# Softmax sums in the slot of their own logits, inverses and scaling half a slot sooner, six buffers for the recurrence's states

## The chip, the cores and the metric

The kernel runs on one core of a Trainium2 chip. The metric is device time in microseconds (us) of one execution; lower is better. The core has five engines with an instruction queue each: TensorE (PE; its weight loads appear as PEld), VectorE (DVE), ScalarE (ACT), GpSimd (POOL) and SyncE (SP), which here issues the DMAs.

## What is computed

The input x is 4 images of 128 channels and 64 x 64 pixels, fp32. Two layers follow each other.

Layer 0: a layernorm over channels, plus a 3x3 depthwise convolution with edge padding (cpe) of the same; then, in windows of 16 x 16 pixels, an attention in which each pixel looks at its 5 x 5 neighbours (zeros outside the window take part in the softmax), in 2 branches of 4 heads with 32 channels; an output projection and the residual.

```python
logits = einsum("nbhdij,nbhdkij->nbhkij", q, k_nb) * scale   # k over 25 neighbours
attn = softmax(logits, axis=3)
o = einsum("nbhkij,nbhdkij->nbhdij", attn, v_nb)
```

Layer 1, on the 4096 tokens of each image: t += cumulative linear attention of layernorm(t), with num = q . cumsum(k v), den = q . cumsum(k) + 1e-6, q and k through elu + 1; then t += recurrence, where layernorm(t) goes through a matrix and a batchnorm, and y = sigmoid(wx_t + y V^T) runs from token to token.

## The kernel before

**Tiles and stages.** The work is 16 bands (4 images x 4 rows of windows, 16 x 64 pixels each) of 4 windows, 64 "places" in all. A loop of 66 slots (lines 705 to 741) goes over the places. Slot i computes `logits(i)`: on PE a mask (L383) and 48 small matmuls (L388) into four banks, on ACT four Exp (L397) into the tiles `es0` to `es3`. Later in the slot `window_inputs` makes q, k (L343, copied from the bank on ACT at L351) and v (L356, L363, with two DMAs that lay v out anew, L365 and L366) of window i + 1.

The window before, i - 1, is finished in three pieces by the generator `weighted`: the softmax denominators as matmuls with ones (L406), their copy `den` (ACT, L409) and a DMA that packs every 32nd row into `dc` (L411); then the weighted values (48 small matmuls, L418) with the copy `o_sb` (ACT, L426); then the inverses on DVE (L429 to L433), a DMA of them to memory (`rd`, L435) and one back, spread over the partitions (`rden`, L437). Window i - 2 is scaled on POOL (`scaled`, L446: oT = o_sb * rden).

**The gaps.** Between these pieces `between(i, gap)`, gap 0 to 5, takes one step of each of two generators. `behind` is layer 1 of the band before, 24 steps (list at L618 to L643) for its two halves a and c: `output0` (output projection L471, residual L478), `measure` (L197, L199 on DVE, L201 and L202 on POOL), `norm` (L209, DVE), `turn` and `turn_last` (transposes, L218), queries, keys and values (L500 to L525, with `low` L502 on ACT, L504 and L505 on DVE), `scores` (L543, L545), `accumulate` (the running state: matmuls L560, additions L568), `attend` (L579, L581; DVE L589 to L593) and `keep` (transposes L218, copy L598, a DMA to memory L599). `product` (L608 to L610) is the matrix of the recurrence. `ahead` is `front`: the layernorm (`norm_rows`) and the convolution of later bands (`convolve`: nine `taps`, L292 on ACT and L294 on DVE, then the copy `y2w` L330 on ACT). Layer 1 of band n begins in slot 4n + 5, and its `keep` of half a falls at gap 2 of slot 4n + 8.

**What sets the order.** `in_order` (L166) ties the instructions of PE, DVE, ACT and POOL, each in the order in which the program writes them. SP is not tied. Every engine therefore waits in program order: an instruction that waits holds all that stand behind it on its engine. Slots 0 to 4 have no layer 1 to run; `ahead` alone fills their gaps. The convolution of the first band's last windows is done on PE (`multiply_first`, L312); `fourth` is the last of it, run in slot 0.

**Buffers.** Pools a1 and a2 have one and two buffers per tag; `y2`, `q`, `k`, `es`, `dc`, `o_sb` and `v_sb` come in two, `den` and `rden` in one. PE writes to 8 banks (pool ps), and a bank is free when an engine has copied what it holds.

**The end.** Slots 64 and 65 and the loop's remainder finish layer 1 of the last band. In slot 65 the pools of layer 0 are closed and `res` (all images but one, 6.3 MB) is loaded from memory for the last step. The recurrence (L826 to L860) runs 42 rounds over segments side by side, each of two halves: PE adds y V^T to a bank (L834), ACT takes the sigmoid (L847) into `ys`, from a ring of three buffers. In the 32 rounds that count POOL adds the residual to 24 of 32 columns and DVE to 8 (L854), and a DMA writes them out (L860). Checks of the recurrence's warm-up follow (L865 to L893).

```python
            sums = weighted(windows[i - 1]) if 1 <= i <= len(places) else iter(())
            for gap in (1, 2):
                next(sums, None)
                between(i, gap)
            run(sums)
```

Of the kernel before, what the change touches and what calls it, by code (L numbers as in the profile page):

```python
# [17 lines left out]
P = 128  # L18
# [28 lines left out]
def conv_attn_hybrid(ctx: ExitStack, tc: tile.TileContext, ins: dict, out: bass.AP):  # L47
# [276 lines left out]
    def convolve(n, half):  # L324

        y = ypads[n] if half == 0 else ypads.pop(n)
        y2 = a2.tile([P, WS, 2 * WS], F32, tag="y2", name="y2")
        yield from taps(y2, y, half * 2 * WS, 2 * WS, 1 + half)
        y2w = a2.tile([P, 2, WT], F32, tag="y2w", name="y2w")
        nc.scalar.copy(  # L330
            y2w.rearrange("p n (r c) -> p n r c", c=WS),
            y2.rearrange("p r (n c) -> p n r c", c=WS),
        )
        y2s[n, half] = y2w

    def window_inputs(w, n, wj):
# [3 lines left out]
        for name, wT in (("q", wqT), ("k", wkT)):  # L340
            pps = bank()
            for br in range(BR):
                nc.tensor.matmul(  # L343
                    pps[:, br * WT : (br + 1) * WT],
                    wT[:, br * P : (br + 1) * P],
                    y2,
                    start=True,
                    stop=True,
                )
            w[name] = a2.tile([P, BR * WT], F32, tag=name, name=name)  # L350
            nc.scalar.copy(w[name], pps)  # L351
            yield
# [46 lines left out]

    def weighted(w):  # L400


        ops, dps = bank(), bank()
        for h in range(HEADS):
# [4 lines left out]
        nc.scalar.copy(den, dps)  # L409
        dc = a2.tile([P, 16], F32, tag="dc", name="dc")  # L410
        nc.sync.dma_start(dc, den[::HD, :])  # L411
        yield
        for br, n in pieces:
            cols, _ = spans(br, n)
            for h in range(HEADS):
# [8 lines left out]
                )  # L424
        o_sb = a2.tile([P, BR * WT], F32, tag="o_sb", name="o_sb")
        nc.scalar.copy(o_sb, ops)  # L426
        yield

        nc.vector.tensor_tensor(dc, dc, pad_c, ALU.add)  # L429
        rc = a2.tile([P, 16], F32, tag="rc", name="rc")  # L430
        nc.vector.reciprocal(rc, dc)
        nc.vector.tensor_tensor(dmax, dmax, dc, ALU.max)
        nc.vector.tensor_tensor(dmin, dmin, dc, ALU.min)  # L433
        rd = dram4.tile([HEADS, BR * WT], F32, tag="rd", name="rd")
        nc.sync.dma_start(rd.rearrange("h (a e) -> (h a) e", e=16), rc)  # L435
        rden = a1.tile([P, BR * WT], F32, tag="rden", name="rden")
        nc.sync.dma_start(rden, rd.unsqueeze(1).to_broadcast([HEADS, HD, BR * WT]))  # L437
        w["o"], w["rden"] = o_sb, rden
        yield

# [111 lines left out]
    def accumulate(h):  # L552

        h.states = [states.get(h.b)]
        for e in range(2):
            dps = bank()
            ds = [dps[:, i * (P + 1) : (i + 1) * (P + 1)] for i in range(2)]
            for i, d in enumerate(ds):
# [4 lines left out]
            for d in ds:  # L563
# [5 lines left out]
                h.states.append(new)  # L569
        states[h.b] = h.states.pop()  # L570

# [133 lines left out]
    for i in range(len(places) + 2):  # L705
        if i < len(places):
            n, wj = places[i]
            if i and wj == 0 and n + 1 < len(bands) and bands[n + 1][1] < NB - 1:
                load_head(n + 2)
            logits(windows[i])  # L710
        if 2 <= i:
            m, wjm = places[i - 2]
            if wjm == NB - 1:
                run(behind)
                behind = layer1(m, halves.pop(m - 1, (None, None)))
        between(i, 0)
        if 2 <= i:
            scaled(m, wjm, windows.pop(i - 2))
        if i == len(places) + 1:
            layer0.close()  # L720
            early = fast.enter_context(tc.tile_pool(name="early", bufs=1))
            res = early.tile([P, B - 1, NH, SEG, HSEGS], F32, name="res")
            for b in range(B - 1):
                nc.sync.dma_start(res[:, b].rearrange("p n s k -> p n (s k)"), resd[b])
        if i < len(places) and wj == 1 and n + 2 < len(bands):
            load(n + 2)
        sums = weighted(windows[i - 1]) if 1 <= i <= len(places) else iter(())
        for gap in (1, 2):
            next(sums, None)
            between(i, gap)  # L730
        run(sums)
        if i == 0:
            run(fourth)
        inputs = iter(())
        if i + 1 < len(places):
            windows[i + 1] = {}
            inputs = window_inputs(windows[i + 1], *places[i + 1])
        for gap in (3, 4, 5):
            next(inputs, None)
            between(i, gap)  # L740
        run(inputs)
    run(behind)
    run(layer1_end(*halves.pop(len(bands) - 1)))
# [68 lines left out]

    last = ring.tile([P, COLS], F32, tag="ys", name="ys")
    for c0, c1 in halves:
# [11 lines left out]
    for r, (s, counts) in enumerate(rounds):  # L826
        seed(r // 2 + ZBUFS - 1, r % 2)

        moved, were_moved = rounds[r] == (SEG - 1, False), rounds[r] == (0, True)
        ys = None if moved else ring.tile([P, COLS], F32, tag="ys", name="ys")  # L830
        for g, (c0, c1) in enumerate(halves):
# [729 lines left out]
```

## Time and profile before

| what | value |
|---|---|
| median of 6 runs | 928.7 us (926.81 to 931.01) |
| the profiled execution | 925.04 us |
| its span, first to last instruction | 923.3 us |
| mean granted PE clock | 0.982 |
| PE, DVE, ACT, POOL busy | 95%, 79%, 58%, 28% of the span |
| first mask matmuls of slots 0 to 4 (L383) | 23.43, 32.71, 39.01, 45.38, 52.15 us |
| logits of slot 5 (L388) | 64.48 us |
| distance of bands (first L471 of a band: 226.14, 276.58, 326.45, 377.25) | some 50.3 us |
| last sums (L406) | 805.86 us |
| first output projection of the last band (L471) | 820.64 us |
| first and last addition of the recurrence on POOL (L854) | 875.00 and 912.7 us |

In the rows that follow, L12 is line 12 of the kernel before. A row has a start in us, a length in us, the engine, the line, the operation, output <- inputs, and how many instructions it gathers; in brackets stands how long the engine had been idle and what ended it. A PE that is "busy" may still run at half clock; the granted clock is a column of its own.

### The profile page before, as it was taken

To read this page: it belongs to the slowest core of one execution; us is meant where nothing else is said; L and a number is where in the kernel's file an instruction comes from. 1 tells how busy PE (TensorE), PEld (TensorE's weight loads), DVE (VectorE), ACT (ScalarE), POOL (GpSimd) and SP (SyncE) were. 2 spreads that over 40 slices of the span, in tenths; PEclk is the share of its full clock that TensorE was granted. 3 is DMA by queue.
4 is the path that set the end of the run, shared out by engine and by line. 5 is a ranking of instruction groups with operands and counts; after the bars stand their busy time and mean duration, and the time that the engine had idled before them with its cause. 6 is when DMAs were issued, how large, how long until landed. Compare 5 with 4: busy or idle time off the path is not lost.

```text
span 923.3 us, 26463 instructions
## 1 busy us (share of the span) xinstructions
PE 872.8 (95%) x10507; PEld 652.0 (71%) x10508; DVE 732.6 (79%) x2408; ACT 539.6 (58%) x1010; POOL 259.7 (28%) x358
## 2 busy tenths in 40 slices
PE   4978999999999999999999999999999999977894
PEld 3756777877777877777787777777777778656452
DVE  6465979888897978798888879787979887577684
ACT  3755566565756565665656575656666565623463
POOL 2122230413232232314132323223231412131195
PEclk9988999999999999999999999999999999999798
DMA  4111121121212111212112121212121111153154
GB/s 122 34 43 56 49 72 37 54 57 58 60 63 57 52 55 49 74 38 72 46 50 61 60 60 49 64 50 67 49 72 38 55 38 49 40 204 154 75 218 150
DMA packets 53189, 63.46 MB, mean 69 GB/s; under 512 B 22976, under 2 KB 33856, under 8 KB 52416
## 3 DMA queue, kind: packets, MB, share of 16 engines
q1 hardware_dynamic: 51616, 61.10, 21.0%
q8 instruction: 85, 1.39, 0.6%
q10 hardware_dynamic: 1440, 0.57, 0.3%
q14 instruction: 48, 0.39, 0.1%
HBM read 35.44 MB, written 17.30 MB: 57 GB/s over the span
## 4 chain that ended last, share of the span: by engine, by line
PE 57%; DVE 28%; ACT 5%; POOL 4%; issue 4%; DMA 2%; ACTq 0%; POOLq 0%; DVEq 0%; SPq 0%
DVE y L294 10%; PE bank L343 8%; PE bank L471 6%; PE bank L388 6%; PE bank L218 6%; PE bank L500 4%; PE bank L406 4%; PE bank L356 4%; PE bank L418 3%; PE bank L608 3%; DVE st L197 2%; PE z L834 2%; DVE f L505 2%; PE bank L579 2%; DVE state L568 2%
## 5 line engine op out<-in xcount | busy, mean ns | idle before, releaser
L294 DVE SCALAR_TENSOR_TENSOR y<-ypad,cpe_w,y 128x512 f32<-128x512 f32 x240 | 192.3, 801 | 15.0 <-ACT y L292 11.5
L397 ACT ACTIVATE es<-bank 128x512 f32<-128x512 f32 x256 | 132.2, 603 | 77.1 <-PE bank L388 77.1
L446 POOL TENSOR_TENSOR oT<-o_sb,rden 128x512 f32<-128x512 f32 x64 | 83.1, 1298 | 244.1 <-DMA rden<-rd 191.2
L201 POOL TENSOR_SCALAR rs<-mv 128x4 f32<-128x4 f32 (+2 forms) x100 | 25.0, 250 | 364.7 <-DVE mv L199 161.2
L209 DVE TENSOR_SCALAR xn<-x,mv,rs 128x128 f32<-128x128 f32 x256 | 90.0, 412 | 26.5 <-POOL rs L202 26.5
L202 POOL TENSOR_TENSOR rs<-rs,mhalf 128x4 f32<-128x4 f32 (+2 forms) x100 | 106.3, 1063 | 8.3
L388 PEld LDWEIGHTS bank<-q,k 32*128 32x128 f32 x3072 | 97.7, 189 | 7.6 <-ACT k L351 6.4
L388 PE MATMUL bank<-q,k 32*128 32x96 f32 (+1 forms) x3072 | 96.3, 270 | 1.1 <-ACT k L351 1.1
L418 PEld LDWEIGHTS bank<-es,v_sb 128*32 128x32 f32 x3072 | 56.6, 110 | 30.2 <-issue 17.1
L471 PE MATMUL bank<-woT,oT 128*128 128x128 f32 x512 | 65.6, 282 | 5.4 <-POOL oT L446 5.4
L500 PE MATMUL bank<-xl,awT 128*128 128x512 f32 x128 | 70.0, 630 | 0.0
L418 PE MATMUL bank<-es,v_sb 128*32 128x96 f32 (+1 forms) x3072 | 69.9, 239 | 0.0
L406 PE MATMUL bank<-es,ones 128*32 128x512 f32 x512 | 69.1, 612 | 0.0
L471 PEld LDWEIGHTS bank<-woT,oT 128*128 128x128 f32 x512 | 62.3, 196 | 9.5 <-POOL oT L446 7.1
L363 ACT COPY v_sb<-bank 128x512 f32<-128x512 f32 x64 | 37.5, 586 | 53.5 <-PE bank L356 46.8
L343 PE MATMUL bank<-y2w,wqT 128*128 128x256 f32 x256 | 66.4, 382 | 1.1 <-DVE y2w L294 1.1
L343 PE MATMUL bank<-y2w,wkT 128*128 128x256 f32 x256 | 65.8, 380 | 0.0
L356 PE MATMUL bank<-wvT,y2w 128*128 128x256 f32 x256 | 65.8, 380 | 0.0
L351 ACT COPY q<-bank 128x512 f32<-128x512 f32 x64 | 37.6, 588 | 41.0 <-PE bank L343 39.0
L351 ACT COPY k<-bank 128x512 f32<-128x512 f32 x64 | 37.4, 584 | 36.8 <-PE bank L343 36.7
L197 DVE BATCH_NORM_STATS2 st<-x 128x6 f32<-128x128 f32 x256 | 55.5, 280 | 1.1
L343 PEld LDWEIGHTS bank<-y2w,wqT 128*128 128x128 f32 x256 | 45.8, 194 | 12.8 <-issue 7.2
(118 smaller groups left out, 1714.0 us busy)
## 6 DMA issues: line engine op xcount, KB each, us to landing
rden<-rd SPq DMA_DIRECT2D x64, 256.0 KB
v_sb<-v_sb SPq DMA_DIRECT2D x128, 64.0 KB
resd<-rs_o SPq DMA_DIRECT2D x32, 256.0 KB
out<-ot SPq DMA_DIRECT2D x32, 256.0 KB
xin<-in_xt SPq DMA_DIRECT2D x15, 512.0 KB
res<-resd SPq DMA_DIRECT2D x3, 2048.0 KB
late<-resd SPq DMA_DIRECT2D x2, 1024.0 KB
dc<-den SPq DMA_DIRECT2D x64, 8.0 KB
```

Source lines behind the costliest of these rows:

```text
L202: nc.gpsimd.tensor_tensor(rs[:, :n], rs[:, :n], mhalf[:, :n], ALU.pow)
L209: nc.vector.tensor_scalar(xn[:, j, :], piece, mv[:, j, 0:1], rs[:, j : j + 1], ALU.subtract, ALU.mult)
L294: nc.vector.scalar_tensor_tensor(y2, src, cpe_w[:, tap : tap + 1], y2, ALU.mult, ALU.add)
L343: nc.tensor.matmul(pps[:, br * WT : (br + 1) * WT], wT[:, br * P : (br + 1) * P], y2, start=True, stop=True,)
L356: nc.tensor.matmul(vps[:, e * 256 : (e + 1) * 256], y2[:, e * P : (e + 1) * P], wvT, start=True, stop=True,)
L388: nc.tensor.matmul(sps[h][:, cols], w["k"][rows, k0 : k0 + P], w["q"][rows, cols], start=False, stop=(br, n) == pieces[-1],)
L397: nc.scalar.activation(es, sps[h], AF.Exp, scale=scale)
L406: nc.tensor.matmul(dps[rows], ones[:, :HD], w["es", h], start=True, stop=True)
L418: nc.tensor.matmul(ops[rows, cols], w["v"][:, n, c0 : c0 + HD], w["es", h][:, cols], start=(br, n) == pieces[0], stop=(br, n) == pieces[-1],)
L446: nc.gpsimd.tensor_tensor(oTs[n][:, :, :, wj * WS : (wj + 1) * WS], w["o"].rearrange("p (a r c) -> p a r c", a=BR, c=WS), w["rden"].rearra ...
L471: nc.tensor.matmul(yps[:, j * P : (j + 1) * P], oT[:, br, t], woT[:, br, :], start=br == 0, stop=br == BR - 1,)
L500: nc.tensor.matmul(zps, awT[:, m * P : (m + 1) * P], h.xl, start=True, stop=True)
```

## The change

`weighted` is cut into three functions. `sums(i)` (denominators, den, dc's DMA) is now called in slot i itself, between gap 2 and the inputs of the next window. `weighted(i - 1)` keeps the weighted values and o_sb and stands between gap 1 and gap 2. `inverses(i)` (DVE, and the two DMAs of rd and rden) stands in slot i behind v of the next window, ahead of gap 5. `scaled(i - 1)` stands in slot i behind gap 4, where `scaled(i - 2)` stood behind gap 0. The pools of layer 0 are so closed, and res loaded, in slot 64 rather than 65. The load of a later band's x keeps its place behind gap 0.

Besides: `y2`, `q` and `k` have one buffer instead of two; `accumulate` leaves out the last of the four state updates in the last half of each image, where nothing reads the state; `ys` has six buffers.

```diff
--- before.py
+++ after.py
@@ -324,7 +324,7 @@
     def convolve(n, half):
 
         y = ypads[n] if half == 0 else ypads.pop(n)
-        y2 = a2.tile([P, WS, 2 * WS], F32, tag="y2", name="y2")
+        y2 = a1.tile([P, WS, 2 * WS], F32, tag="y2", name="y2")
         yield from taps(y2, y, half * 2 * WS, 2 * WS, 1 + half)
         y2w = a2.tile([P, 2, WT], F32, tag="y2w", name="y2w")
         nc.scalar.copy(
@@ -347,7 +347,7 @@
                     start=True,
                     stop=True,
                 )
-            w[name] = a2.tile([P, BR * WT], F32, tag=name, name=name)
+            w[name] = a1.tile([P, BR * WT], F32, tag=name, name=name)
             nc.scalar.copy(w[name], pps)
             yield
         vps = bank()
@@ -397,19 +397,35 @@
             nc.scalar.activation(es, sps[h], AF.Exp, scale=scale)
             w["es", h] = es
 
-    def weighted(w):
-
-
-        ops, dps = bank(), bank()
+    def sums(w):
+
+        dps = bank()
         for h in range(HEADS):
             rows = slice(h * HD, (h + 1) * HD)
             nc.tensor.matmul(dps[rows], ones[:, :HD], w["es", h], start=True, stop=True)
 
         den = a1.tile([P, BR * WT], F32, tag="den", name="den")
         nc.scalar.copy(den, dps)
-        dc = a2.tile([P, 16], F32, tag="dc", name="dc")
-        nc.sync.dma_start(dc, den[::HD, :])
-        yield
+        w["dc"] = a2.tile([P, 16], F32, tag="dc", name="dc")
+        nc.sync.dma_start(w["dc"], den[::HD, :])
+
+    def inverses(w):
+
+        dc = w["dc"]
+
+        nc.vector.tensor_tensor(dc, dc, pad_c, ALU.add)
+        rc = a2.tile([P, 16], F32, tag="rc", name="rc")
+        nc.vector.reciprocal(rc, dc)
+        nc.vector.tensor_tensor(dmax, dmax, dc, ALU.max)
+        nc.vector.tensor_tensor(dmin, dmin, dc, ALU.min)
+        rd = dram4.tile([HEADS, BR * WT], F32, tag="rd", name="rd")
+        nc.sync.dma_start(rd.rearrange("h (a e) -> (h a) e", e=16), rc)
+        w["rden"] = a1.tile([P, BR * WT], F32, tag="rden", name="rden")
+        nc.sync.dma_start(w["rden"], rd.unsqueeze(1).to_broadcast([HEADS, HD, BR * WT]))
+
+    def weighted(w):
+
+        ops = bank()
         for br, n in pieces:
             cols, _ = spans(br, n)
             for h in range(HEADS):
@@ -422,21 +438,8 @@
                     start=(br, n) == pieces[0],
                     stop=(br, n) == pieces[-1],
                 )
-        o_sb = a2.tile([P, BR * WT], F32, tag="o_sb", name="o_sb")
-        nc.scalar.copy(o_sb, ops)
-        yield
-
-        nc.vector.tensor_tensor(dc, dc, pad_c, ALU.add)
-        rc = a2.tile([P, 16], F32, tag="rc", name="rc")
-        nc.vector.reciprocal(rc, dc)
-        nc.vector.tensor_tensor(dmax, dmax, dc, ALU.max)
-        nc.vector.tensor_tensor(dmin, dmin, dc, ALU.min)
-        rd = dram4.tile([HEADS, BR * WT], F32, tag="rd", name="rd")
-        nc.sync.dma_start(rd.rearrange("h (a e) -> (h a) e", e=16), rc)
-        rden = a1.tile([P, BR * WT], F32, tag="rden", name="rden")
-        nc.sync.dma_start(rden, rd.unsqueeze(1).to_broadcast([HEADS, HD, BR * WT]))
-        w["o"], w["rden"] = o_sb, rden
-        yield
+        w["o"] = a2.tile([P, BR * WT], F32, tag="o_sb", name="o_sb")
+        nc.scalar.copy(w["o"], ops)
 
     oTs = {}
 
@@ -552,9 +555,10 @@
     def accumulate(h):
 
         h.states = [states.get(h.b)]
+        count = 4 - (h.hb == NH - 1)
         for e in range(2):
             dps = bank()
-            ds = [dps[:, i * (P + 1) : (i + 1) * (P + 1)] for i in range(2)]
+            ds = [dps[:, i * (P + 1) : (i + 1) * (P + 1)] for i in range(min(2, count - 2 * e))]
             for i, d in enumerate(ds):
                 j = 2 * e + i
                 nc.tensor.matmul(
@@ -567,7 +571,7 @@
                 else:
                     nc.vector.tensor_tensor(new, h.states[-1], d, ALU.add)
                 h.states.append(new)
-        states[h.b] = h.states.pop()
+        states[h.b] = h.states[-1]
 
     def attend(h, e):
 
@@ -703,7 +707,8 @@
             next(ahead, None)
 
     for i in range(len(places) + 2):
-        if i < len(places):
+        inside, after = i < len(places), 1 <= i <= len(places)
+        if inside:
             n, wj = places[i]
             if i and wj == 0 and n + 1 < len(bands) and bands[n + 1][1] < NB - 1:
                 load_head(n + 2)
@@ -714,31 +719,36 @@
                 run(behind)
                 behind = layer1(m, halves.pop(m - 1, (None, None)))
         between(i, 0)
-        if 2 <= i:
-            scaled(m, wjm, windows.pop(i - 2))
-        if i == len(places) + 1:
-            layer0.close()
-            early = fast.enter_context(tc.tile_pool(name="early", bufs=1))
-            res = early.tile([P, B - 1, NH, SEG, HSEGS], F32, name="res")
-            for b in range(B - 1):
-                nc.sync.dma_start(res[:, b].rearrange("p n s k -> p n (s k)"), resd[b])
-        if i < len(places) and wj == 1 and n + 2 < len(bands):
+        if inside and wj == 1 and n + 2 < len(bands):
             load(n + 2)
-        sums = weighted(windows[i - 1]) if 1 <= i <= len(places) else iter(())
-        for gap in (1, 2):
-            next(sums, None)
-            between(i, gap)
-        run(sums)
+        between(i, 1)
+        if after:
+            weighted(windows[i - 1])
+        between(i, 2)
+        if inside:
+            sums(windows[i])
         if i == 0:
             run(fourth)
         inputs = iter(())
         if i + 1 < len(places):
             windows[i + 1] = {}
             inputs = window_inputs(windows[i + 1], *places[i + 1])
-        for gap in (3, 4, 5):
-            next(inputs, None)
-            between(i, gap)
+        next(inputs, None)
+        between(i, 3)
+        next(inputs, None)
+        between(i, 4)
+        if after:
+            scaled(*places[i - 1], windows.pop(i - 1))
+        if i == len(places):
+            layer0.close()
+            early = fast.enter_context(tc.tile_pool(name="early", bufs=1))
+            res = early.tile([P, B - 1, NH, SEG, HSEGS], F32, name="res")
+            for b in range(B - 1):
+                nc.sync.dma_start(res[:, b].rearrange("p n s k -> p n (s k)"), resd[b])
         run(inputs)
+        if inside:
+            inverses(windows[i])
+        between(i, 5)
     run(behind)
     run(layer1_end(*halves.pop(len(bands) - 1)))
     in_order(first)
@@ -810,7 +820,7 @@
     nc.gpsimd.memset(warm[:, :, 0:1], 0.0)
     halves = [(0, GC), (GC, COLS)]
 
-    last = ring.tile([P, COLS], F32, tag="ys", name="ys")
+    last = ring.tile([P, COLS], F32, tag="ys", name="ys", bufs=6)
     for c0, c1 in halves:
         nc.scalar.activation(
             last[:, c0:c1].rearrange("p (m k) -> p m k", k=HSEGS),
@@ -827,7 +837,7 @@
         seed(r // 2 + ZBUFS - 1, r % 2)
 
         moved, were_moved = rounds[r] == (SEG - 1, False), rounds[r] == (0, True)
-        ys = None if moved else ring.tile([P, COLS], F32, tag="ys", name="ys")
+        ys = None if moved else ring.tile([P, COLS], F32, tag="ys", name="ys", bufs=6)
         for g, (c0, c1) in enumerate(halves):
             b = slice(c0 // SEGS, c1 // SEGS)
             z = seeds[r // 2, g][:, r % 2, :]
```

## The prediction

> **What bounds the kernel now.** I read the busy shares first, then TensorE (PE) by windows of time, then the rows in which PE waited, then the queue of VectorE (DVE) and GpSimd (POOL) round the two long waits, and the chain of waits for the end.
>
> ```profile
> PE 872.8 (95%) x10507; PEld 652.0 (71%) x10508; DVE 732.6 (79%) x2408; ACT 539.6 (58%) x1010; POOL 259.7 (28%) x358
> ```
>
> The windows, each with its length, then busy time (and count) of PE, weight loads, DVE, ScalarE (ACT) and POOL, the granted PE clock, DMA share and GB/s:
>
> ```profile
> 40.00:65.00 25.00, 19.82 (x348) 14.30 (x348) 15.97 (x42) 15.52 (x30) 4.50 (x5) 0.93 0.18 51
> 65.00:100.00 35.00, 32.66 (x419) 24.03 (x412) 21.22 (x64) 19.50 (x36) 8.23 (x12) 0.86 0.17 53
> ...
> 300.00:400.00 100.00, 99.21 (x1286) 76.05 (x1285) 84.86 (x288) 61.71 (x113) 28.44 (x41) 1.00 0.19 55
> ...
> 600.00:700.00 100.00, 99.94 (x1287) 76.09 (x1286) 85.14 (x287) 62.21 (x114) 27.55 (x38) 1.00 0.19 56
> ...
> 800.00:840.00 40.00, 33.09 (x304) 25.01 (x301) 30.34 (x106) 12.71 (x22) 8.58 (x11) 1.00 0.47 186
> ```
>
> Between 100 and 800 us PE is the bound: the seven windows leave 3.5 us idle. There a change pays only if it removes matmuls, and costs as soon as it makes PE wait. Room lies at both ends. PE's rows at its longest waits (start, length, line; in brackets the idle time and its releaser):
>
> ```profile
> 63.02 0.58 PE L383 MATMUL bank<-mask_q,mask_k 32*128 32x512 bf16 x1 [4.12 <-ACT den L409]
> 64.48 2.89 PE L388 MATMUL bank<-q,k 32*128 32x96 f32 x48 [0.88 <-ACT k L351]
> ...
> 74.83 3.63 PE L471 MATMUL bank<-woT,oT 128*128 128x128 f32 x16 [2.34 <-POOL oT L446]
> ```
>
> ```profile
> 820.64 2.05 PE L471 MATMUL bank<-woT,oT 128*128 128x128 f32 x16 [2.47 <-POOL oT L446]
> ```
>
> POOL's rows before the last of them:
>
> ```profile
> 818.35 1.01 POOL L202 TENSOR_TENSOR rs<-rs,mhalf 128x4 f32<-128x4 f32 x1
> 819.33 1.26 POOL L446 TENSOR_TENSOR oT<-o_sb,rden 128x512 f32<-128x512 f32 x1
> ```
>
> The scaling of window 63 sits behind a layernorm's power (L202) in POOL's order, although its inverses were issued long before.
>
> **The change, part by part** (against the profiled execution, 925.04 us; span 923.3 us. The median of the six runs, 928.7, is 3.7 above it, and I add that at the end.)
>
> *Start-up, slots 0 to 5.* Here nothing of layer 1 fills PE. Removed: the 4.12 us are not a wait for the sums as such. ACT runs its list in order; y2w (L330) stands in front of den, o_sb and the q, k, v copies, and waits 5.87 us for the convolution taps on DVE (L294), which end at 61.83. A bank for the mask matmul comes free only when den is copied. After, the same copies still stand behind y2w. Moreover DVE reaches the taps later: the inverses of the slot's own window stand in DVE's order before the last gap's taps, and wait for a dc that was issued only behind the previous window's rden on SP. In the rows before, dc lands 1.9 us after issue when alone (62.99 to 64.86) and about 4 us after it when behind an rden (43.37 to 47.18); DVE's three waits for it before 62 us are 0.83, 2.41 and 3.14. I get taps that end at 64.0 to 64.3, 2.3 later. Added: PE's sums now need the slot's own Exp. Four Exp take 2.06 us from 0.1 us behind the logits. In slot 0 only 18 convolution matmuls (25.06 to 29.14) could cover them, and these stand behind the sums, so PE waits about 1.65; in slots 1 to 4 the 1.07 us of weighted matmuls and little else lie between, which leaves about 0.6 in each: 4 us together, most of which shortens the wait for the taps that follows. Gained: oT of window 3 is no longer late, so the 2.34 us go, and with them part of the slow clock. From 63.02 to 78.25 PE took 15.2 us, of which 3.2 idle in the two waits at 64.48 and 74.83 and 6.9 the work of those blocks at full-speed durations (L388 1.48 for 2.89, L406 1.06 for 1.94, L471 2.05 for 3.63): 5.1 us are the clock. If logits of slot 5 start at about 67 (64.48 + 2.3) with PE warm, PE reaches the place of 78.25 at 76.6; with another cold stretch at 78.1, or, if dc lands still later, at 81. I take **0** (bounds -3 and +3): a later start traded for a warm clock and a wait removed.
>
> The granted clock in 2 us rows was 0.50 from 62 to 70 after the wait of 4.12, 0.50 at 76 to 78 after the one of 2.34, and 1.00 right through the one of 2.47 at 818 to 820.6. The Trainium skill ("TensorE: Matmul & The Clock Gate", section "What's actually happening") says that the clock halves after an idle window of some 3.4 us and that the window runs free. By that rule waits split into pieces of 0.6 would never cool PE, and the start-up term here would be -1.6 rather than 0; the row with 0.50 after only 2.34 speaks against counting on it.
>
> *The middle, slots 6 to 63.* Removed: the last of four state updates in the last half of each batch (4 times): two passes of 0.13 us each on PE, 4 x 2 x 0.13 = 1.06 us, of which one lies in the tail: **-0.8**. Its DVE additions (0.29 each) lie beside PE. Three waits of 0.21 for oT (175.87, 377.25, 578.43): **-0.6**. Moved: the sums (8 passes, 1.06 us) go from behind gap 0 to behind gap 2 of the slot. They are covered by everything between, because Exp ends 2.1 us after the logits and gaps 0, 1 and weighted hold over 3 us of PE. But in the fourth slot of a band gap 2 is where `keep` of half a turns x; PE meets it 1.06 us earlier, and its wait for x from DVE, already there, grows:
>
> ```profile
> 363.98 0.58 PE L218 MATMUL bank<-ident,x 128*128 128x128 f32 x2 [0.35 <-DVE x L593]
> ```
>
> DVE is unbroken from 350.82 to 376, so x comes sooner only by what its start gains: `low` at 350.82 waited 1.80 for ACT, where den's copy (0.6) stood directly ahead. It gains about 0.5, so PE loses 1.06 - 0.5 = 0.55 a band. Against that, the inverses (366.79 to 367.24, 0.45 us on DVE) no longer stand ahead of xn (L209), for which the transposes at 368.98 took 1.01 rather than 0.60: -0.45 a band. Over 14 bands 14 x 0.1 = **+1.4**. SP: rden's issues go behind v_sb's, so v, read a whole slot later, lands sooner; the scaling that reads rden has half a slot from there. y2, q and k with one buffer each: their readers (y2w's copy, the logits) stand before the next writer in every order, so 0; if not, one ACT copy of 0.59 per slot would show. Middle: 0.0 (bounds -3 and +4; for +10 see the rivals).
>
> *The tail, from the last logits on.* PE loses sums(63) from 805.86 (0.99 to the next start) and DVE the inverses at 810.77 (1.49 to the next start, slow because POOL's L446 of 810.65 runs beside it). State L568, behind those inverses, held PE 0.48 at 812.60 and xn 0.90 at 813.99. So x of half c, ended at 816.93, ends 2 us sooner; oT(63) is scaled a slot sooner and its place on POOL is free, so output0 follows the product instead of waiting 2.47. What is late next is DVE: statistics, rs (1.3), xn (1.11 alone, not the 2.04 it took beside the scaling), statistics L610 (0.69), then x15 at 819.1 to 819.5 instead of 822.73: **-3.3** (bounds -1.5 and -4.5; the loads of res, 6.3 MB, start a slot sooner, and in SP's order stand before the stores of the last rows, which are not due before 841.98). The fourth skipped update: **-0.3**. The rest up to the recurrence is one chain, which moves as a whole.
>
> *The recurrence.* Rounds start 1.17 us apart until ACT's wait for the ring begins, then 1.22. In front of these sigmoids stands an event wait:
>
> ```profile
> L847 ACTq EVENT_SEMAPHORE  x29: 642/788/790, 876.9 to 911.0; - x29
> ```
>
> With six buffers its readers are older, but the instruction still names POOL and PE, so one such wait stays. The least gain is three rounds that begin without it, 3 x 0.05 = 0.15, the most 29 x 0.045 = 1.3. POOL's addition (1.10 a round) fits below 1.17 too. **-0.4**, nearer the lower end, because ACT at 877.58 started before DVE's addition of 877.31 had ended, so the readers were not what held it.
>
> Sum: 0 + 0.0 - 3.3 - 0.3 - 0.4 = -4.0: 925.04 becomes 921.0, and the median 928.7 - 4.0 = **924.7 us**.
>
> **Rivals.** *A, the start-up gains too.* PE stays warm, both long waits go, slot 5 is reached as early as 61: -3 there, -1.3 in the recurrence, -4.5 at the tail: 917 to 921 in runs. For it: 7.3 us of idle and 5.1 of slow clock lie there. Against: the taps, which set the 4.12, do not move earlier.
>
> *B, no change that can be measured.* The measurement tells some 0.3% (2.8 us) from nothing. The later taps cost 2 to 3 us in full while the tail gives 3: 926 to 930, at 928. For it: DVE's waits for dc are in the rows of before already; the changed order adds one queue ahead of dc.
>
> *C, slower: `keep` meets DVE.* If `low` does not move by 0.5 (ACT's Exp hold it instead) and POOL's scaling, now in gap 4 or 5, slows DVE's inverses as it did at 810.77 (1.18 for 0.14), every band costs the full 1.06 on PE: 14 x 1.06 = +14.8, less 0.45 x 14 = 6.3 and less 0.8 + 0.6 + 4.0 in the rest: about +3; with the collision of 1.04 in one window of each band +14 x 0.5 more: **932 to 939**, at 935. It decides as soon as the wait at `keep` exceeds 0.9 us a band. Against: DVE has 14 to 15 us of slack in each 100.
>
> *D, six buffers do not do what they say*: the round stays at 1.22. That costs the forecast 0.4 and no more; it is within its range.
>
> **How the numbers follow.** Forecast 0.42 (922 to 927), A 0.18, B 0.20, C 0.20. Limits are 925.9 and 931.5. Faster: 0.75 of the forecast and all of A: 0.50. Same: the rest of the forecast and 0.9 of B: 0.28. Slower: C and the rest: 0.22. The range leaves out the lower tenth (half of A) and the upper (half of C): 918 to 934.
>
> **What would show it.** Right: PE's wait at `keep` of half a is 0.7 to 1.1 a band, and the transposes of `turn_last` take 0.6; no PE wait for oT is left; in the first 62 us PE waits for ACT's es in front of the sums, 1.6 once and about 0.6 in four slots; the taps before slot 5 end at 64; the first output0 of the last band starts at 816 to 817. Wrong: band starts more than 0.3 us further apart than 50.3 (rival C), a wait on PE for es or dc after slot 6, or rounds at 1.17 throughout (recurrence -1.3).

## The result: 934.0 us, slower where a small gain was forecast

The changed kernel's median is 934.02 us over 18 runs (930.08 to 938.39); the kernel before, run beside it, has 928.57 us over 39 (925.61 to 931.73). The ratio is 1.0058, 95% interval 1.0045 to 1.007: about 5.4 us lost, where 4.0 were to be won. Two more measurements gave 1.005 (1.003 to 1.0069) and 1.0088 (1.0058 to 1.0117). The profiled execution took 939.66 us, with a span of 937.6.

The windows of the changed kernel's trace (length; busy time and count of PE, weight loads, DVE, ACT, POOL; granted PE clock; DMA share; GB/s), to set beside those of before:

```profile
40.00:65.00 25.00, 25.00 (x392) 16.23 (x380) 14.21 (x23) 17.87 (x34) 3.58 (x3) 1.00 0.17 45
65.00:100.00 35.00, 30.38 (x371) 22.61 (x371) 24.67 (x82) 18.73 (x34) 10.51 (x15) 0.95 0.18 53
...
300.00:400.00 100.00, 97.21 (x1254) 74.62 (x1256) 82.13 (x279) 59.34 (x110) 28.02 (x41) 0.98 0.18 54
...
600.00:700.00 100.00, 98.78 (x1279) 75.09 (x1271) 83.86 (x283) 62.04 (x114) 26.46 (x38) 1.00 0.19 56
...
800.00:840.00 40.00, 37.58 (x453) 28.91 (x451) 26.38 (x100) 17.90 (x32) 9.62 (x13) 1.00 0.26 92
```

PE is no longer full in the middle: from 100 to 800 us it is busy 685.8 us instead of 696.6. The new idle time is nearly all in one place. PE's rows there in two bands of the changed kernel:

```profile
270.03 0.59 PE L218 MATMUL bank<-ident,x 128*128 128x128 f32 x2 [1.35 <-DVE x L597]
...
680.12 0.59 PE L218 MATMUL bank<-ident,x 128*128 128x128 f32 x2 [0.45 <-DVE x L597]
```

This is `keep` of half a, at gap 2 of a band's fourth overlapped slot: PE wants to turn x, which DVE has not finished. It waited 0.2 to 0.44 us there before. In the changed kernel the waits of 0.2 us and more sum to 14.0 us over the bands, against 2.4 before.

Stage by stage I use four marks: slot 0's first mask matmul, the first output projection of band 1, of band 14 and of band 15. "Before's order" are the kernel before and three kernels below that keep its order of the sums; "changed" are three profiles of the changed kernel.

| stage | before's order (4 profiles) | changed (3 profiles) | difference of means |
|---|---|---|---|
| slot 0 to band 1 | 101.6 to 104.0 | 102.8, 102.9, 103.1 | +0.2 |
| band 1 to band 14 | 649.9 to 653.1 | 666.7, 664.4, 664.6 | +13.7 |
| band 14 to band 15 | 42.1 to 43.2 | 39.3, 39.3, 39.3 | -3.5 |
| band 15 to the end of the span | 102.7 to 106.4 | 103.6, 103.4, 103.7 | -0.3 |

The stages sum to some 10 us, the timed runs to 5.4 to 8 or so. The three profiled executions of the changed kernel (939.66, 937.87, 937.93 us) lie 3 to 6 us above their timed medians, those of before's order between 3.5 below and 3 above. Why is open; the stages show where time goes, the ratios how much.

### The profile page after: what moved, and what is told of

Its sections match the earlier page's. It is cut to its first block, busy times and chain, and to the rows that moved or that the text cites. A ratio compares the mean times of both kernels' runs of the same rounds, so it can differ in the third digit from the quotient of the medians.

```text
span 937.6 us, 26498 instructions
## 1 busy us (share of the span) xinstructions
PE 882.0 (94%) x10499; PEld 655.1 (70%) x10500; DVE 733.2 (78%) x2404; ACT 539.2 (58%) x1010; POOL 254.8 (27%) x358
## 4 chain that ended last, share of the span: by engine, by line
PE 77%; DVE 16%; issue 2%; ACT 2%; DMA 1%; POOL 1%; ACTq 0%; DVEq 0%; POOLq 0%
PE bank L343 12%; PE bank L405 8%; PE bank L218 7%; PE bank L388 7%; PE bank L503 6%; PE bank L474 6%; DVE y L294 6%; PE bank L434 6%; PE bank L356 5%; PE z L844 4%; PE bank L612 3%; PE bank L520 3%; PE bank L546 2%; PE bank L383 2%; DVE x L597 2%
## 5 line engine op out<-in xcount | busy, mean ns | idle before, releaser
L294 DVE SCALAR_TENSOR_TENSOR y<-ypad,cpe_w,y 128x512 f32<-128x512 f32 x240 | 197.9, 825 | 12.0 <-ACT y L292 9.0
L209 DVE TENSOR_SCALAR xn<-x,mv,rs 128x128 f32<-128x128 f32 x256 | 82.0, 382 | 32.0 <-POOL rs L202 31.9
L202 POOL TENSOR_TENSOR rs<-rs,mhalf 128x4 f32<-128x4 f32 (+2 forms) x100 | 98.9, 989 | 8.3
L405 PE MATMUL bank<-es,ones 128*32 128x512 f32 x512 | 76.3, 617 | 0.7 <-ACT es L397 0.7
L343 PE MATMUL bank<-y2w,wqT 128*128 128x256 f32 x256 | 74.7, 415 | 1.0 <-DVE y2w L294 1.0
L503 PE MATMUL bank<-xl,awT 128*128 128x512 f32 x128 | 67.6, 612 | 0.0
L474 PE MATMUL bank<-woT,oT 128*128 128x128 f32 x512 | 64.7, 280 | 0.0
L474 PEld LDWEIGHTS bank<-woT,oT 128*128 128x128 f32 x512 | 61.8, 194 | 3.6 <-issue 0.8
L408 ACT COPY den<-bank 128x512 f32<-128x512 f32 x64 | 37.9, 592 | 40.3 <-PE bank L405 39.3
```

The lines of the kernel that those rows point to most:

```text
L202: nc.gpsimd.tensor_tensor(rs[:, :n], rs[:, :n], mhalf[:, :n], ALU.pow)
L209: nc.vector.tensor_scalar(xn[:, j, :], piece, mv[:, j, 0:1], rs[:, j : j + 1], ALU.subtract, ALU.mult)
L294: nc.vector.scalar_tensor_tensor(y2, src, cpe_w[:, tap : tap + 1], y2, ALU.mult, ALU.add)
L343: nc.tensor.matmul(pps[:, br * WT : (br + 1) * WT], wT[:, br * P : (br + 1) * P], y2, start=True, stop=True,)
L405: nc.tensor.matmul(dps[rows], ones[:, :HD], w["es", h], start=True, stop=True)
L474: nc.tensor.matmul(yps[:, j * P : (j + 1) * P], oT[:, br, t], woT[:, br, :], start=br == 0, stop=br == BR - 1,)
```

## The experiments

**The changed kernel twice more**, for further profiles (no edit).

> The changed kernel once more, for a second profile. Theory K (PE meets keep of half a 1.06 us earlier in each band and waits for x from DVE): ratio to before 1.004 to 1.008, PE's wait at keep summed over the bands 8 to 14 us, and a wait over 1.2 us followed now and then by a stretch at half clock, which would explain why the profiled run (939.66) lies 5.6 above the median. Theory S (the loss is in the start-up, slots 0 to 5): the wait at keep differs from run to run and does not carry the difference; the start-up is 5 us or more later than before.

> The changed kernel a third time, for its profile: PE's wait at keep summed over the bands 8 to 16 us, from 0.3 to 1.4 in a band; the bands with 1.2 us or more are those in which POOL's scaling starts inside a pair of taps of that slot (2.4 us for the pair instead of 1.53). Rival: the sum is under 6 us where the execution takes 934 or less.

Medians 934.66 and 935.03 us. The waits at `keep` of 0.2 us and more sum to 15.3 and 14.3 us (the first profile, 14.0): 1.0 to 1.1 in a band. The rival of few waits is out. The start-up theory is out by the table. What sets the wait's size is seen in DVE's rows ahead of `keep`. First the band with the long wait, then one with the short, both from the changed kernel:

```profile
256.56 0.43 DVE L507 TENSOR_SCALAR low<-low 128x512 f32<-128x512 f32 x1 [0.67 <-ACT low L505]
...
257.69 1.53 DVE L294 SCALAR_TENSOR_TENSOR y<-ypad,cpe_w,y 128x512 f32<-128x512 f32 x2
259.69 0.69 DVE L528 TENSOR_TENSOR v<-bank,abv 128x512 f32<-128x512 f32 x1 [0.47 <-PE bank L520]
260.30 2.45 DVE L294 SCALAR_TENSOR_TENSOR y<-ypad,cpe_w,y 128x512 f32<-128x512 f32 x2
```

```profile
667.75 0.43 DVE L507 TENSOR_SCALAR low<-low 128x512 f32<-128x512 f32 x1 [0.67 <-ACT low L505]
...
670.70 0.69 DVE L528 TENSOR_TENSOR v<-bank,abv 128x512 f32<-128x512 f32 x1 [0.30 <-PE bank L520]
671.31 1.53 DVE L294 SCALAR_TENSOR_TENSOR y<-ypad,cpe_w,y 128x512 f32<-128x512 f32 x2
```

Two things differ: the wait of `v` for PE (0.47 and 0.30), and a pair of taps that takes 2.45 us instead of 1.53. The slow pair lies beside POOL's scaling, which starts when rden lands (260.94 to 262.20 here; in the second band at 672.82, behind the taps). In the first and third profiles of the changed kernel all 15 waits of 1.0 us or more go with a pair of 2.08 to 2.63 us, and the shorter ones with pairs of 1.53 to 2.07; in the second one wait of 1.18 goes with 2.04. This tells the long waits from the short ones, not the changed kernel from the kernel before: there the pair beside POOL took 2.2 to 2.6 us in each of the eight bands whose wait shows. Only the last band waits 0.31 with 2.42: no statistics of a later band stand between the two additions of x there.

The expectation also linked long waits to half clock. Only some show it. The changed kernel's windows after the wait of 1.36 us that ended at 321.61:

```profile
320.00:322.00 2.00, 0.64 (x4) 0.33 (x3) 1.93 (x14) 0.09 (x1) 0.91 (x2) 1.00 0.24 85
322.00:324.00 2.00, 2.00 (x10) 0.36 (x11) 2.00 (x13) 0.62 (x2) 1.25 (x3) 0.59 0.30 114
324.00:326.00 2.00, 2.00 (x7) 1.64 (x8) 0.25 (x4) 0.58 (x2) 1.82 (x4) 0.55 0.22 75
```

The granted clock falls to about half for some 3.4 us and the band takes 52.67 us; after the wait of 1.35 at 270.03 it stayed at 1.00. Of 20 waits of 1.3 us or more in the three profiles, three had such a stretch behind them (two, none and one), so it is a small part of the loss.

**Sums ahead of gap 2**, so that PE does them before it comes to `keep`, as it did before:

```diff
         if after:
             weighted(windows[i - 1])
-        between(i, 2)
         if inside:
             sums(windows[i])
+        between(i, 2)
```

> The changed kernel with sums(i) ahead of gap 2 instead of behind it, so that PE again does the sums before it turns x for keep. Theory K: PE's wait at keep of half a falls back to 0.2 to 0.5 us a band (from 1.0 on average), 0.7 to 1.0 x 14 = 10 to 14 us less than the changed kernel in the profile, 918 to 925 us, faster than before. Theory S: no change against the changed kernel, 931 to 935.

918.03 us, ratio 0.986 (0.9832 to 0.9887). One pair of lines turns +0.6% into -1.4%: 16 us. The waits at `keep` fall to 6.3 us in all, as theory K said, yet they are not what was won, since 6.7 us of new waits for xn stand at `turn_last`. Between the marks of band 1 and band 14 PE is idle for 11.5 us, against 12.9 to 14.6 in the three profiles of the changed kernel, and busy for 636.3 us, against 649.8 to 653.3. So the time came where K put it for another reason: in the profile PE's matmuls took some 13 us less. That is the theory W of a later run: sums now stand directly behind the weighted matmuls, both with 32-column weights. PE's rows in this kernel:

```profile
229.09 1.09 PE L434 MATMUL bank<-es,v_sb 128*32 128x96 f32 x48
230.00 1.04 PE L405 MATMUL bank<-es,ones 128*32 128x512 f32 x8
230.97 2.05 PE L474 MATMUL bank<-woT,oT 128*128 128x128 f32 x16
232.86 1.03 PE L343 MATMUL bank<-y2w,wqT 128*128 128x256 f32 x4
```

and the same stretch of the changed kernel:

```profile
230.39 1.09 PE L434 MATMUL bank<-es,v_sb 128*32 128x96 f32 x48
231.41 2.05 PE L474 MATMUL bank<-woT,oT 128*128 128x128 f32 x16
233.39 1.06 PE L405 MATMUL bank<-es,ones 128*32 128x512 f32 x8
234.39 1.13 PE L343 MATMUL bank<-y2w,wqT 128*128 128x256 f32 x4
```

From start to start, q's matmuls take 0.86 us behind other 128-column work and 0.96 behind the sums (234.39 to the next row at 235.35): 0.1 us for the passage out of small weights (a passage is a change between groups with 32-column or 32-row weights and groups with 128x128 ones). L474 stands behind small weights in both kernels, and in the changed kernel ahead of them too: 1.98 instead of 1.89, so 0.09 for the passage into them. With those of the logits a band has 16 passages here and 24 in the kernel before and the changed one. Over the 13 bands between the marks that is 104 fewer, some 10 of the 13 us.

**`keep` one step later**, with the sums where the change has them:

```diff
-            (scores, c), (keep, a), None,
-            (accumulate, c), (norm, a), None,
+            (scores, c), None,
+            (accumulate, c), (norm, a), (keep, a), None,
```

> The changed kernel with keep of half a one step of layer 1 later (with accumulate c and norm a, gap 3 instead of gap 2); the sums stay behind gap 2 and so come before keep. Theory K: the wait at keep is gone (below 0.2 a band) with the sums where the change put them, 10 to 14 us less in the profile, 918 to 925. A rival K2 (not keep's place but the sums' own wait or switch on PE costs the time): the time stays within 2 us of the changed kernel's, 932 to 936.

928.68 us, ratio 0.9994 (0.9973 to 1.0015). No wait at `keep` is left, and about 6 us are regained, not 10 to 14. K2 is out, and K holds with a smaller size: `turn_last` waits for xn instead, up to 0.89 us in a band (all waits shown sum to 6.3), since DVE is not done sooner. The middle takes 657.4 us, half way between 665 and 652; PE is idle for 6.6 us of it and busy for 650.8.

**The pair behind gap 2, with `keep` late**: `keep_late` with weighted moved from ahead of gap 2 to directly ahead of the sums.

```diff
         between(i, 1)
+        between(i, 2)
         if after:
             weighted(windows[i - 1])
-        between(i, 2)
         if inside:
             sums(windows[i])
```

> The changed kernel with keep of half a one step later (as in keep_late) and weighted(i - 1) moved behind gap 2, directly ahead of sums(i), so that the two groups of 32-column matmuls are one group in each slot. Theory K alone (the wait at keep is the whole loss of the middle): the same as keep_late, 927 to 930. Theory K + W (each passage between 32-column and 128-column weights costs PE about 0.1 us; two fewer in a slot, 8 fewer in a band): 1.0 to 1.4 us a band less than keep_late without PE's waits, 14 x 1.0 to 1.4 = 14 to 20 less if no new wait appears, 910 to 918.

920.49 us, ratio 0.9913 (0.9887 to 0.9939): 8 us better than `keep_late`, less than the 14 to 20. K alone is out. In the middle PE is busy for 639.2 us instead of 650.8: 11.6 us for 104 passages, or 0.11 for one, as the rows above have it. Its idle time grows from 6.6 to 13.7 us, most of it for xn, so some 60% of what the passages save is given back to DVE. W holds, at some 0.1 us a passage; why PE takes that time, no run shows.

**Sums behind q and gap 3.** PE reaches `keep` as early as in the changed kernel, but L520, for which DVE's `v` waits, comes sooner (5.97 us behind its slot's masks instead of 7.16).

```diff
         between(i, 2)
-        if inside:
-            sums(windows[i])
...
         next(inputs, None)
         between(i, 3)
+        if inside:
+            sums(windows[i])
```

> The changed kernel with sums(i) one step later still, behind q and gap 3 of the slot (and in slot 0 behind fourth). PE turns x for keep at the same place as in the changed kernel, ahead of the sums, but reaches the values of half c (L520), for which DVE's v has to wait 0.3 to 0.7 us a band in the changed kernel and not at all before, 1.06 us sooner. Theory V (low's 0.5 us on DVE were gained as predicted and then lost again in this wait): v's wait for L520 goes, x comes 0.5 us sooner and PE's wait at keep falls to 0.4 to 0.9 a band; with the first slots' sums behind q (3 us) some 5 to 9 us less than the changed kernel, 925 to 929. Rival: x does not move, since the taps beside POOL's scaling set it; the wait at keep stays at 1.0 on average, 931 to 935.

924.86 us, ratio 0.998 (0.9963 to 0.9997); the changed kernel, measured beside it, had 1.0088. The wait lists (total, times, longest) have the wait of `v`, first the changed kernel's, then this one's:

```profile
DVE v L528 <- PE bank L520: 11.3, 16, 1.8
```

```profile
DVE v L528 <- PE bank L520: 2.3, 2, 1.7
```

In the middle, waits at `keep` fall from 14.3 to 7.1 us with the slow taps still there (2.1 to 2.6 us in all ten bands shown). So theory V holds: the wait of `v` for PE, not POOL's collision alone, keeps x late. No run takes the collision away, so what it adds to the other half is not shown. The first slots changed too (sums behind q), but the first stage takes 102.4 us, hardly less; the middle takes 653.1.

**Ahead's steps at odd gaps**, in the changed kernel:

```diff
-        if i < len(places) and (i == 0 or i % NB or gap in (0, 2, 4)):
+        if i < len(places) and (i == 0 or i % NB or gap in (1, 3, 5)):
```

> The changed kernel, sums where it has them, with the steps of ahead in the first slot of a band taken at gaps 1, 3 and 5 instead of 0, 2 and 4. The statistics of a later band's x (L197 and L199, 1.2 us on DVE) then stand behind the second addition of attend a instead of ahead of it. Theory K (what PE waits for at keep is DVE's queue): the wait at keep falls by 1.0 to 1.2 us a band to at most 0.3, 12 to 14 us less in the middle, 920 to 925. Rival: DVE is late at the next place by as much (turn_last's xn behind the same statistics), so the wait only moves there and the time stays within 3 us of 934.

934.79 us, ratio 1.0047 (1.0031 to 1.0063): as the rival said. The wait at `keep` falls as K said, to 0.3, and a new one stands 10 us later. PE's rows:

```profile
267.00 0.59 PE L218 MATMUL bank<-ident,x 128*128 128x128 f32 x2 [0.31 <-DVE x L597]
...
276.94 1.00 PE L218 MATMUL bank<-ident,xf 128*128 128x128 f32 x4 [0.45 <-DVE xf L209]
```

The waits shown in the middle sum to 10.0 us instead of 14: 4.8 for xf, 1.8 for x, and 3.3 that the profile puts down to ACT's Exp. The time is the changed kernel's. A piece of DVE's queue moved only moved the wait.

**The first slots' sums later**, on top of sums ahead of gap 2, and the same with ahead's steps at odd gaps (`best_odd`, which adds the edit just shown):

```diff
-        between(i, 2)
-        if inside:
+        if inside and 5 <= i:
             sums(windows[i])
+        between(i, 2)
         if i == 0:
             run(fourth)
+            sums(windows[i])
...
         next(inputs, None)
+        if 1 <= i < 5:
+            sums(windows[i])
         between(i, 3)
```

> sums_before_gap2 with the sums of slot 0 behind the last convolution matmuls (fourth) and those of slots 1 to 4 behind q of the next window, so that PE has work while ACT takes Exp. Theory X (PE's waits for es in the first five slots, seen as sums of 2.3 to 2.5 us instead of 1.06, some 7.8 us together, set when slot 5 begins): logits of slot 5 start 3 us or more sooner, 914 to 916. Theory T (the convolution taps on DVE set it, through y2w on ACT): PE waits longer ahead of slot 5's masks instead and slot 5's logits move by less than 2 us, 916.5 to 919.

> start_later with the same move of ahead's steps. Theory K: the wait of 0.5 to 1.0 at keep goes, 0.4 to 0.6 a band, 5 to 9 us less than start_later, 907 to 911. Rival (the wait moves to turn_last's xn, which already waits 0.35 to 0.7 a band): within 2 us of start_later, 914 to 918.

915.82 us, ratio 0.9871 (0.9835 to 0.9908), and 914.84 us, ratio 0.9828 (0.98 to 0.9857). Against sums ahead of gap 2 (0.986) `start_later` is not distinct. Its logits of slot 5 start 42.0 us after slot 0's masks instead of 45.2, while PE waits 2.66 instead of 0.36 at the masks of slot 5: X and T both see part of what happens. `best_odd` is where its rival put it. These are the fastest kernels of the study, 1.3 to 1.7% below the kernel before.

**Parts alone, on the kernel before.** Six buffers:

```diff
-    last = ring.tile([P, COLS], F32, tag="ys", name="ys")
+    last = ring.tile([P, COLS], F32, tag="ys", name="ys", bufs=6)
...
-        ys = None if moved else ring.tile([P, COLS], F32, tag="ys", name="ys")
+        ys = None if moved else ring.tile([P, COLS], F32, tag="ys", name="ys", bufs=6)
```

> The kernel before with six buffers for ys and nothing else. My prediction's step: 0.15 to 1.3 us less, rounds still with an event wait ahead of most sigmoids. Rival: nothing (rounds at 1.22 after the warm-up, as before), or all of it (rounds of 1.17 throughout, 1.3 us less). All three lie within 0.2%: the time alone will not tell, the spacing of the sigmoids will.

928.03 us, ratio 0.9982 (0.9967 to 0.9997). The interval just excludes no gain, yet the trace shows no place for 1.6 us: rounds start 1.17 us apart until the ring wait begins, then 1.23 to 1.24, where the three-buffer ring had 1.22 to 1.23. The row of the sigmoids' event wait, of this kernel:

```profile
L847 ACTq EVENT_SEMAPHORE  x26: 17/17/17, 887.1 to 918.2; - x26
```

The wait is met at once (17 ns), yet each round is 0.06 longer from its first use on. That points to the further wait itself as the price, not to a reader that is late; no run takes the wait away. Three fewer such rounds save 0.15, and 26 that are 0.01 longer cost 0.3.

The skipped update:

```diff
+        count = 4 - (h.hb == NH - 1)
...
-            ds = [dps[:, i * (P + 1) : (i + 1) * (P + 1)] for i in range(2)]
+            ds = [dps[:, i * (P + 1) : (i + 1) * (P + 1)] for i in range(min(2, count - 2 * e))]
...
-        states[h.b] = h.states.pop()
+        states[h.b] = h.states[-1]
```

> The kernel before with the fourth state update left out in the last half of each image, nothing else. My prediction's step: PE 8 passes of 0.13 us fewer, 1.1 us less in all (ratio 0.9988). Rival: nothing, since DVE or the tail's chain hides it (ratio 1.000). They lie 0.12% apart, so the time may not decide; the bands that hold an image's last half should be 0.27 us shorter than the others by their output projections.

926.64 us, ratio 0.9989 (0.9968 to 1.0011). The middle value is the one forecast, but the interval holds the rival too; the time did not decide. The bands with a last half (from bands 3, 7 and 11 to the next) took 49.8 us on average, and 50.4 in the kernel before; that leans to the step, but bands scatter by as much.

The scaling sooner:

```diff
         between(i, 0)
-        if 2 <= i:
-            scaled(m, wjm, windows.pop(i - 2))
...
-        for gap in (3, 4, 5):
+        for gap in (3, 4):
             next(inputs, None)
             between(i, gap)
+        next(inputs, None)
+        if 1 <= i <= len(places):
+            scaled(*places[i - 1], windows.pop(i - 1))
...
+        between(i, 5)
         run(inputs)
```

> The kernel before with the scaling alone moved: scaled(i - 1) behind gap 4 and v of slot i instead of scaled(i - 2) behind gap 0 of the next, and res loaded one slot sooner; sums, inverses and all else as before. My prediction's step on the tail: most of the 3.3 us come from oT(63) being ready, so the first output projection of the last band starts 1.5 to 3 us sooner, and the three 0.2 us waits for oT go: 925.5 to 928. Rival: rden lands after the scaling's new place and holds POOL, and with it the layernorms' rs behind it: the middle gets longer, 929 to 934.

928.09 us, ratio 0.9997 (0.9975 to 1.0018). The tail still waits, as PE's row shows:

```profile
822.51 3.39 PE L471 MATMUL bank<-woT,oT 128*128 128x128 f32 x16 [2.02 <-POOL oT L446]
```

The stage is 42.1 us, 1.1 less than the kernel before's 43.2, not 39.3. The tail's gain in the changed kernel is therefore not the scaling's place alone. The skipped update alone has 42.7 there; for the rest the sums and inverses out of slot 64 are what is left, and no run moves them by themselves. POOL was not held by it in the middle (650.9 us).

## Why the prediction was wrong, point by point

**The step that failed: the middle, forecast 0.0, and in it the +1.4 of 14 bands x (1.06 - 0.5 - 0.45).** The middle measured +13.7 us in the profiles. The place was named, PE at `keep` of half a, and the sign given for it even came true: the wait is 1.0 to 1.1 a band, within 0.7 to 1.1. So did the sign of rival C, since bands start 51.1 to 51.3 us apart on average. In the timed runs, which lost 5.4 us in all, the middle must be smaller: an estimate is 5.4 + 3.6 for the tail, some 9 us. What went wrong is the price. The row of before that the forecast started from, 0.35, was one of the longer ones (2.4 us in 14 bands is 0.17 a band), so the wait grew by 0.83 to 0.92 a band and not by 0.55, and the 0.45 that was to pay for it did not come.

The first half of the working held. In the band read here (masks of the slot ahead of `keep` at 244.91 us before, at 251.44 after) PE came to `keep` 16.84 us behind these masks instead of 18.03: the sums' 1.0 from start to start, and two passages. `low` on DVE started 0.48 us sooner (5.60 us behind its slot's masks before, 5.12 after) where 0.5 were forecast. The failure is in "x comes sooner only by what its start gains. It gains about 0.5". Between `low` and x stands `v`, which reads PE's L520, and L520 sits 7.15 us behind its slot's masks in both kernels. DVE, 0.48 sooner, waited there 0.47. DVE's rows of before, to set beside the first ones of the changed kernel above:

```profile
251.64 2.42 DVE L294 SCALAR_TENSOR_TENSOR y<-ypad,cpe_w,y 128x512 f32<-128x512 f32 x2
...
254.46 0.68 DVE L525 TENSOR_TENSOR v<-bank,abv 128x512 f32<-128x512 f32 x1
...
263.11 0.61 DVE L593 SCALAR_TENSOR_TENSOR x<-bank,rd,x 128x128 f32<-128x128 f32 x2
```

I had taken DVE to be unbroken because its rows of before showed no wait; they showed none because the slow pair of taps and the inverses stood ahead of `v`, which started 9.55 us behind the masks when L520 had been done for 1.3 us. With both behind it, `v` came early enough to wait: in the changed kernel it starts 8.25 us behind its slot's masks in all 14 bands, after a wait of 0.30 to 0.67. So x came 18.81 us behind those masks before and 18.79 after in this band; over the bands with statistics between the additions it came at 18.3 to 19.0 before and at 17.9 to 19.0 after. The run that shows it is the sums behind gap 3: the wait of `v` gone, half of the waits at `keep` gone.

The credit of -0.45 a band at `turn_last` is the larger part of the miss. Its transposes take 0.74 us in place of 1.01 in the bands read here, -0.27, but the next ones are longer: x of half c takes 0.86 where it took 0.66, and xf 0.92 where it took 0.60. Between the marks of band 1 and band 14 the forecast comes to some 7 us more idle time on PE and 7 us less work. On average PE's idle time grew by 10.9 us (from 2.2 to 3.3 up to 12.9 to 14.6), and its busy time by 2.8 (from 647.3 to 649.8 up to 649.8 to 653.3, the stretches at half clock included). `keep_late` and ahead's steps show why no such credit is safe: what is spared at one of PE's reads of DVE is waited for at the next.

**Rival C was the outcome**, at 0.20: PE's earlier coming lost at `keep`, 932 to 939 forecast, 934.0 measured. Its condition "if `low` does not move" was wrong; `low` moved, and the gain was lost behind it. Its second part, POOL's scaling beside DVE, is there, but it slows taps (2.45 for 1.53) and not the inverses, and the kernel before pays it too (2.42 for a pair at 251.64). C also took off 6.3 us for `turn_last` that did not come, so that its range holds the time is in part luck.

**The start-up, forecast 0: right as a sum (+0.2) by luck, since its terms were wrong and cancelled.** PE's waits for Exp are 2.1 us in slot 0 (0.68 idle, and L405 2.45 from start to start for 1.0) and 1.3 in each of slots 1 to 4 (2.28 for 1.0): some 7.3, not 4. They hide in the row's length, since the matmuls of a row wait one by one. The taps ended at 67.2, not 64, because DVE waited 6.07 and 1.92 us for dc. Yet the clock held, and the wait of 4.12 ahead of slot 5 shrank to 1.09 at its logits. The 2.34 us for oT went, but 3.53 for xf came in (at 75.54), since DVE's inverses ahead of it waited 2.77 for dc. The rule that the Trainium skill gives for the clock ("TensorE: Matmul & The Clock Gate", section "What's actually happening": an idle window of some 3.4 us, free-running) would let all those pieces through at full clock, and this stage agrees: the clock is 1.00 up to 76 us, and 0.66 and 0.50 in the 2 us rows behind the 3.53. The 1.36 us at 321.61, followed by half clock, does not fit an idle window of that length; the measurement decides.

**The tail, forecast -3.6 with the skipped update: right in size.** Band 14 to band 15 is 3.5 us shorter. The first output projection follows the product with no wait for oT, and xn is late next (2.11 us), as forecast:

```profile
833.11 1.02 PE L612 MATMUL bank<-xl,fwT 128*128 128x512 f32 x2
833.97 1.95 PE L474 MATMUL bank<-woT,oT 128*128 128x128 f32 x16
...
840.75 1.15 PE L218 MATMUL bank<-ident,xn 128*128 128x128 f32 x4 [2.11 <-DVE xn L209]
```

**The recurrence, forecast -0.4:** at best nothing; rival D was right.

**The chances.** The seven windows had shown that PE has nothing to win in the middle and DVE 85% busy beside it. With 14 repetitions of a wait priced by a small difference of larger numbers (1.06 - 0.5 - 0.45), its sign was open, and C deserved more than 0.20.

## What to carry to other kernels

- An engine that shows no wait in a stretch may meet another one as soon as its work is moved: `v` had L520's result 1.3 us before it ran, and waited 0.47 us for it after. Before an earlier start is booked through to the end of a stretch, list every read in it from another engine, and how long its source had been done at the place where the read will stand.
- Work that fills the bound engine ahead of a repeated meeting with another engine is cover. Moving it behind the meeting can cost its whole length in each repetition, unless the other engine is early by that much; here 0.83 to 0.92 of 1.06 us showed as longer waits.
- Where groups of matmuls with small and with full weights alternate, put the small ones together. Here two passages fewer in a slot were worth as much as the wait that this study set out to explain.

## What the runs showed of the hardware that was not expected

- A passage between matmuls with 32-column weights and those with 128-column weights cost PE about 0.1 us (q 0.96 for 0.86, L474 1.98 for 1.89, from start to start; 11.6 us of busy time for 104 passages).
- A wait of PE for one operand after the other inside a group does not show as idle time: eight L405 passes took 2.35 us instead of 1.06 with no idle time in front, while ACT's Exp made the tiles they read.
- Of 20 waits of PE of 1.3 us or more, three were followed by some 3.4 us at half clock.
- Two 128x512 additions-with-scale on DVE took 2.4 to 2.6 us instead of 1.53 beside POOL's 128x512 product.
- An event wait of 17 ns in front of a sigmoid went with rounds of 1.23 us instead of 1.17.
